# The first sweep of a gated cross-attention block: a listed prologue, a subtraction on GpSimd and a later making of media tiles

## The chip, the cores and the metric

The kernel runs on one core of one Trainium2 chip. The metric is device time in microseconds (us) of one execution, the median of several runs. In what follows PE is TensorE (the matrix engine), DVE is VectorE, ACT is ScalarE, POOL is GpSimd, and SP is the engine that issues most DMAs.

## What is computed

The reference puts four residual blocks behind one another on x of 4 x 1024 x 1024. Only the first matters here, with the layer norm ahead of it:

```python
xb = x.reshape(E, M, K // BLK, BLK)                  # BLK = 128
amax = jnp.max(jnp.abs(xb), axis=-1, keepdims=True)
safe = jnp.maximum(amax, ACT_EPS)
q = (xb * (FP8_MAX / safe)).astype(jnp.float8_e4m3fn)
xq = (q.astype(jnp.float32) * (safe / FP8_MAX)).reshape(E, M, K)
# wq: the same for the media, with one amax for each block of 128 x 128
return jnp.einsum('emk,enk->emn', xq, wq)
...
x = x + jnp.tanh(g_xattn[0]) * _L0_xattn_ref(_layernorm(x, axis=-1), ctx_2048)
```

Both operands of a product of 1024 x 1024 x 1024 (one for each of four batches) are rounded to an 8-bit float and scaled back. Then come a ternary linear layer with an 8-bit activation, whose scale is a maximum over all of x, an attention on the same media, and a layer of eight experts.

## The kernel before, in words

The first sweep (lines 165 to 664) does the first block. It has 32 row tiles of 128 rows of x (class `Rows`, x0 to x31) and 32 media tiles of 128 rows of media, turned (class `Media`, m0 to m31). Eight of each belong to a batch: a row tile of batch b needs all eight media tiles of b, since they hold the output's columns, 128 each.

A **media tile** goes through these steps. `range` is a DVE maximum of each block (L259) and a PE transposition of it (L264). `largest` is a small DVE maximum and a small tensor_scalar (L270, L272) and a PE matmul that spreads the result (L274). `scales` is three or four small DVE instructions (L279 to L285) and one on POOL (L287). Then the tile's sizes: `magnitude` is one ACT instruction (L291), `scale` is eight scaled copies and one Abs on ACT (L221, L230), for tiles that are `scaled`. `round` (function `add`) rounds to the 8-bit float by adding a number of the right size and subtracting it again: k16 by L203 in eight parts or by L197 in one, the sum y by L208 in eight parts (which scales too) or by L199 in one, and last the subtraction, q = y - k16, by L213. `store` writes q, scaled back, into the operand wq: some of the eight blocks by ACT (L237), the rest by DVE (L241). `load` fetches a tile through SP.

A **row tile** has `sum` (ACT, L320), `mean` (DVE, L324), `square` (ACT, L329), `variance` and `range` (DVE L335 and L342, POOL L133 and L347), `scales` (DVE L354, POOL L356 to L358), `scale` (ACT L225 and L230), `round` as above (L197, L199, L213), `restore` (ACT L237 into hd), `transpose` (PE L375), `take` (ACT L381) and `product` in two halves of 512 columns (PE L388, eight matmuls each, which the profile shows as two records each). Then `residual` (DVE L397, which stores x1 and needs the tanh of a gate from `constants`), `spread` (ACT L407), `factor` (DVE L417, POOL L133) and, in every second tile of the first three batches, `extreme` (DVE L426); the other tiles of those come back later (`late_extreme`).

The order on PE, DVE, ACT and POOL is the order in which the program calls these functions: the sweep stands under a manual schedule, and each engine takes its instructions in that order. A prologue (lines 589 to 653) makes up media tiles 0 to 7 in pairs, row tile 0 up to the first half of its product, row tile 1 up to its rounding, and begins row tiles 2 and 3. Then `step(t)` (L517) runs for t = 0 to 31: it does the product of row t, restores row t+1, scales and rounds row t+2, and does the first sums of rows t+3 and t+4. In the first 24 steps it makes up media tile t+8: range and largest one step earlier, scales and round in step t, store in step t+1. PE's `transpose` of the block maxima and its matmul of the largest stand between and behind the halves of the product, so PE waits there for DVE. After step 3 `clear` (L487) fills two buffers by POOL memsets (L490, L495) and writes them out.

Of the first eight media tiles the even ones are scaled; every rounding's subtraction is on DVE; a store of them leaves one of eight blocks to DVE, of the later ones four.

Of the kernel before, what the change touches and what calls it, by code (L numbers as in the profile page):

```python
# [53 lines left out]
def flamingo_kernel(  # L54
# [110 lines left out]
    with ExitStack() as s1:  # L165
# [18 lines left out]
        class Fp8:  # L184


            def tiny(self, name):
                return small.tile(
                    [P, NB], F32, tag=f"{name}{self.name[0]}", name=f"{name}_{self.name}"
                )  # L190

            def add(self, sizes, src, up=None):

                name = self.name
                k16 = w1.tile([P, D], BF16, tag="k16", name=f"k16_{name}", bufs=1)
                if up is None:
                    nc.vector.tensor_scalar(k16, sizes, FP8_LIFT, FP8_FLOOR, ALU.mult, ALU.max)  # L197
                    y = src
                    nc.vector.tensor_tensor(y, src, k16, ALU.add)  # L199
# [12 lines left out]
                self.q = w1.tile([P, D], BF16, tag=f"q{name[0]}", name=f"q8_{name}")  # L212
                nc.vector.tensor_tensor(self.q, y, k16, ALU.subtract)  # L213

            def spread_out(self, src, scale, bias=None):

                name = self.name
                self.y = w1.tile([P, D], F32, tag=f"y{name[0]}", name=f"y8_{name}", bufs=1 + (name[0] == "w"))
# [26 lines left out]
        class Media(Fp8):  # L245


            def __init__(self, t):
                self.t, self.name = t, f"w{t}"

                self.scaled = t < TPB and t % 2 == 0

            def load(self):
                self.c = w1.tile([P, D], F32, tag="c", name=f"c_{self.t}", bufs=4)
# [47 lines left out]
            def store(self):  # L302
                b, hf, j = self.t // TPB, self.t % TPB // NH, self.t % NH
                if (b, hf) not in wqs:
                    wqs[b, hf] = wqp.tile([P, NB, HALF], F32, tag="wq", name=f"wq_{b}_{hf}")
                self.dequantize(wqs[b, hf][:, :, cols(j)], 4 if b else 1)

        class Rows(Fp8):


            def __init__(self, t):
                self.t, self.name = t, f"x{t}"

            def load(self):
                self.x = w1.tile([P, D], F32, tag="x", name=f"x_{self.t}", bufs=6)
# [67 lines left out]
            def product(self, hf):  # L383
# [3 lines left out]
                for k in range(NB):  # L387
# [2 lines left out]
                        start=(k == 0), stop=(k == NB - 1),  # L390
                    )

            def residual(self):
                t = self.t
                self.x1 = w1.tile([P, D], F32, tag="x1", name=f"x1s_{t}")
                tot = small.tile([P, 1], F32, tag="totr", name=f"tot_r{t}")
                nc.vector.scalar_tensor_tensor(  # L397
                    self.x1, self.pm, tg_x0, self.x, ALU.mult, ALU.add, accum_out=tot
                )
                nc.sync.dma_start(x1_dram[t], self.x1)  # L400
                self.mean1 = mean_all[:, t : t + 1]
                nc.vector.tensor_scalar(self.mean1, tot, 1.0 / D, None, ALU.mult)
# [57 lines left out]
        def ternary_scale():  # L460
            tot = small.tile([P, 1], F32, tag="wtot", name="wtot", bufs=1)
            nc.vector.tensor_reduce(tot, part, AX.X, ALU.add)

            spread = w1.tile([P, P], F32, tag="k16", name="wtot_rows", bufs=1)
# [45 lines left out]
        def constants():  # L510
# [3 lines left out]
            nc.scalar.activation(tg, gates, AF.Tanh)  # L514
            nc.scalar.activation(gamma_2, gamma_sb, AF.Square)

        def step(t):  # L517

            near, new, ahead, far, past, old = (at(rows, t + i) for i in (1, 2, 3, 4, -1, -2))
            mp, m, mr, mn = (at(media_t, t + TPB + i) for i in (-1, 0, 1, 3))
# [5 lines left out]
            if t:  # L528
                rows[t].product(0)
            if near:  # L530
                near.restore()
            if mp and t:
                mp.store()
            if ahead:
                ahead.square()
            if past:
                past.residual()
            if mr:
                mr.range()
# [5 lines left out]
            if m:  # L545
                m.scales()
                m.round()
            if old:
                old.factor()
                if old not in waiting:  # L550
                    old.extreme()
# [6 lines left out]
            if mr:  # L558
                mr.largest()
            if past:  # L560
                past.spread()
            if mr:
                mr.magnitude()
            if far:
                far.sum()
            if at(rows, t + 5):
                rows[t + 5].load()
            if mn:
                mn.load()
# [14 lines left out]
            if 5 <= last:  # L584
                for j in range(3 * (last - 5), min(3 * (last - 4), NB)):
                    ternary_block(j)

        with tc.manual_schedule(engines=ORDERED):
# [4 lines left out]
            for r in rows[1:5]:  # L593
                r.load()
            media_t[0].range()
            rows[0].sum()
            rows[0].mean()
            rows[0].square()
            media_t[1].range()
            for m in media_t[0:2]:  # L600
                m.largest()
                m.scales()
            media_t[1].magnitude()
            media_t[0].scale()
            rows[0].variance()
            rows[0].range()
            for i in range(TPB // 2):
                m, n = media_t[2 * i : 2 * i + 2]
                nexts = media_t[2 * i + 2 : min(2 * i + 4, TPB + 1)]
                n.round()  # L610
                if i == 0:
                    rows[0].scales()
                    rows[0].scale()
                elif i == 1:
                    rows[1].sum()
                elif i == 2:
                    rows[1].scales()
                    rows[1].scale()
                else:
                    rows[2].sum()  # L620
                n.store()
                nexts[-1].magnitude()
                for j in nexts:
                    j.range()
                if i in (1, 3):
                    rows[(i + 1) // 2].mean()
                    rows[(i + 1) // 2].square()
                m.round()
                m.store()
                for j in range(2 * i + 4, min(2 * i + 6, TPB + 3)):  # L630
                    media_t[j].load()
                for j in nexts:
                    j.largest()
                if i < 3:
                    for j in nexts:
                        j.scales()
                    nexts[0].scale()
                if i == 0:
                    rows[0].round()
                    rows[0].restore()  # L640
                    rows[0].transpose()
                    rows[0].take()
                elif i == 1:
                    rows[1].variance()
                    rows[1].range()
                    rows[0].product(0)
                elif i == 2:
                    rows[1].round()
                else:
                    rows[2].variance()  # L650
                    rows[2].range()
                    rows[3].sum()
            constants()
            for t in range(NT):
                step(t)
                if t == 3:
                    clear()
# [968 lines left out]
```

## Time and profile before

| | us |
|---|---|
| median of 3 runs | 2051.18 (2050.14 to 2052.25) |
| the profiled execution | 2066.43 |
| its span | 2064.7 |
| PE busy in the span | 1953.8 |
| DVE busy | 1682.4 |
| ACT busy | 1429.4 |
| POOL busy | 600.5 |
| matmuls of the first product (L388), first to last start | 41.8 to 551.8 |

The busy time of an engine is a sum over the whole span; the first sweep is its first quarter. In the lists of single instructions a line gives the start, the duration, engine, line, operation, output and inputs, shape and number; several alike instructions are merged into one line. In the chain of waits a line gives start, length and what the time was spent on. A program's times in the profile come from one execution, which here took longer than the median of the runs.

### The profile page before, as it was taken

Reading aid. Unit: us, or ns where it says so; the run is one execution under the profiler, and the core shown is the slowest. Engines: PE = TensorE matmul, PEld = TensorE weight load, DVE = VectorE, ACT = ScalarE, POOL = GpSimd, SP = SyncE. Lnnn points to the kernel's source line nnn. Section 1 sums busy time; section 2 is a strip of 40 time slices with the busy share of each in tenths; the row PEclk is TensorE's granted clock in tenths of the full one; section 3 lists DMA queues with packets and bytes.
Section 4 is the critical chain, followed back from the end, with each engine's and each line's share of the span. In section 5 each row is a group of like instructions: output and inputs, shape, how many; then the busy total and the mean of one; then the engine's idle time right before and its main releaser. Section 6 shows DMA issues by size and latency. Waiting matters only on the chain.

```text
span 2064.7 us, 24994 instructions
## 1 busy us (share of the span) xinstructions
PE 1953.8 (95%) x7200; PEld 1042.9 (51%) x7200; DVE 1682.4 (81%) x3527; ACT 1429.4 (69%) x2378; POOL 600.5 (29%) x926
## 2 busy tenths in 40 slices
PE   3599999999889999999999999999999999999998
PEld 1244444444334444444444444444444457777766
DVE  8999999988778989898989898989898856555545
ACT  7988988888467776767676777767676645555544
POOL 2234333333100111111212121212121236556664
PEclk9799999999999999999999999999999999999999
DMA  4242332352286767677676767676767865746884
GB/s 173 69 150 98 112 103 92 113 202 102 100 211 159 181 182 182 180 181 187 177 191 174 194 172 194 170 192 172 192 172 184 212 177 195 261 173 212 284 293 162
DMA packets 124751, 357.77 MB, mean 173 GB/s; under 512 B 30583, under 2 KB 38775, under 8 KB 124614
## 3 DMA queue, kind: packets, MB, share of 16 engines
q1 hardware_dynamic: 95094, 271.78, 47.8%
q0 software_dynamic: 29520, 84.39, 12.1%
q8 instruction: 58, 0.95, 0.2%
q14 instruction: 79, 0.65, 0.1%
HBM read 164.08 MB, written 75.61 MB: 116 GB/s over the span
## 4 chain that ended last, share of the span: by engine, by line
PE 86%; DVE 5%; issue 4%; ACT 2%; POOL 2%; DMA 1%; SPq 1%; another core or an unknown queue 0%; POOLq 0%; DVEq 0%; ACTq 0%
PE av L912 21%; PE sc L832 21%; PE mm L388 20%; PE dn L1364 5%; PE f L793 5%; PE up L1374 4%; PE pr L970 3%; PE pt_hmT L960 1%; PE ptx L375 1%; PE pt_hg_acc L1335 1%; PE pt_hg_pt L1335 1%; PE ptq L785 1%; DVE nmax L837 1%; ACT e L841 1%; DVE rmax_w L259 0%
## 5 line engine op out<-in xcount | busy, mean ns | idle before, releaser
L832 PE MATMUL sc<-kv,q 128*128 128x512 f32 x1024 | 488.0, 599 | 4.1 <-ACT q L820 2.4
L912 PE MATMUL av<-eT_x,vT 128*128 128x512 f32 x1008 | 477.3, 596 | 7.7 <-issue 7.5
L388 PE MATMUL mm<-wq,hT 128*128 128x512 f32 x1024 | 454.7, 598 | 0.0
L841 ACT ACTIVATE e<-sc,nmax 128x1024 f32<-128x1024 f32 x256 | 285.3, 1114 | 243.5 <-DVE nmax L837 240.4
L837 DVE TENSOR_REDUCE nmax<-sc 128x1 f32<-128x1024 f32 x256 | 311.9, 1218 | 74.5 <-PE sc L832 74.2
L847 ACT ACTIVATE e<-e,rden 128x1024 f32<-128x1024 f32 x256 | 294.1, 1149 | 58.9 <-DVE rden L844 52.7
L860 DVE STREAM_TRANSPOSE sq<-e 128x1024 f32<-128x1024 f32 x252 | 310.8, 1234 | 0.1
L912 PEld LDWEIGHTS av<-eT_x,vT 128*128 128x128 f32 x1008 | 189.3, 190 | 237.6 <-issue 236.5
L388 PEld LDWEIGHTS mm<-wq,hT 128*128 128x128 f32 x1024 | 191.6, 192 | 220.9 <-issue 217.2
L832 PEld LDWEIGHTS sc<-kv,q 128*128 128x128 f32 x1024 | 185.6, 191 | 182.8 <-issue 169.9
L1364 PEld LDWEIGHTS dn<-hgT,arena_w 128*128 128x128 f32 x1216 | 148.6, 194 | 50.4 <-issue 32.6
L1364 PE MATMUL dn<-hgT,arena_w 128*128 128x128 f32 x1216 | 151.7, 278 | 12.9 <-ACT hgT L1339 10.0
L133 POOL TENSOR_TENSOR rstd_c<-ve_c,neg_half 128x1 f32<-128x1 f32 x31 | 17.7, 570 | 497.4 <-DVE nrm L977 440.8
L1374 PE MATMUL up<-arena_w,ygT 128*128 128x512 f32 x304 | 143.8, 596 | 0.0
L793 PE MATMUL f<-wb_sb 128*128 128x512 bf16 x496 | 117.2, 379 | 2.6 <-DVE y L801 1.4
L1369 ACT COPY ygT<-dn 128x128 f32<-128x128 f32 x76 | 20.3, 267 | 130.0 <-PE dn L1364 97.0
L225 ACT ACTIVATE y_x<-x,off_x,up_x 128x128 f32<-128x128 f32 x256 | 101.5, 479 | 11.5 <-POOL off_x L357 11.5
L237 ACT ACTIVATE hd<-q_x,down_x 128x128 f32<-128x128 bf16 x256 | 78.1, 388 | 21.6 <-DVE q_x L213 21.4
L793 PEld LDWEIGHTS <-wb_sb 128*128 128x128 bf16 x496 | 48.5, 98 | 81.6 <-issue 36.1
L1052 POOL DMA_INDIRECT lists<-token,slot x64 | 66.7, 1042 | 67.3 <-DVE slot L1045 56.8
L133 POOL TENSOR_TENSOR a_all<-va,neg_half 128x1 f32<-128x1 f32 x32 | 36.2, 1131 | 153.1 <-DVE va L417 95.0
L133 POOL TENSOR_TENSOR y<-ve_d,neg_half 128x1 f32<-128x1 f32 x32 | 18.4, 574 | 206.9 <-issue 157.1
(291 smaller groups left out, 2995.5 us busy)
## 6 DMA issues: line engine op xcount, KB each, us to landing
eT_x<-sq SPq DMA_DIRECT2D x1008, 128.0 KB
x<-y SPq DMA_DIRECT2D x32, 514.0 KB
c<-in_ctx_t_dram SPq DMA_DIRECT2D x32, 512.0 KB
x<-in_x_dram SPq DMA_DIRECT2D x32, 512.0 KB
x<-x1s SPq DMA_DIRECT2D x32, 512.0 KB
y<-x SPq DMA_DIRECT2D x32, 512.0 KB
kv<-in_ctx_dram SPq DMA_DIRECT2D x32, 512.0 KB
vT<-in_ctx_t_dram SPq DMA_DIRECT2D x32, 512.0 KB
```

Source lines behind the costliest of these rows:

```text
L225: nc.scalar.activation(self.y[:, cols(k)], src[:, cols(k)], AF.Identity, bias=bias[:, k : k + 1], scale=scale[:, k : k + 1],)
L237: nc.scalar.activation(dst[:, k, :], self.q[:, cols(k)], AF.Copy, scale=down)
L388: nc.tensor.matmul(self.pm[:, hf * HALF : (hf + 1) * HALF], self.hT[:, k, :], wq[:, k, :], start=(k == 0), stop=(k == NB - 1),)
L793: nc.tensor.matmul(po, self.qT[:, k, :], w0T[:, k, cols], start=(k == 0), stop=(k == NB - 1),)
L832: nc.tensor.matmul(sc[:, halves(nh)], qs[t][:, mb * P : (mb + 1) * P], kv[:, halves(nh)], start=True, stop=True,)
L837: nc.vector.tensor_reduce(nmax, sc, AX.X, ALU.max, negate=True)
L841: nc.scalar.activation(self.e, sc, AF.Exp, bias=nmax, accum_out=self.den)
L847: nc.scalar.activation(self.e, self.e, AF.Copy, scale=self.rden)
L860: nc.vector.transpose(sq[:, :, :, j, :], self.e.rearrange("p (k q a) -> p q k a", k=NB, q=4))
L912: nc.tensor.matmul(out_ap, vTs[t][:, k, :], weights, start=(k == 0), stop=(k == NB - 1))
L1364: nc.tensor.matmul(po, self.wa[:, k, :], self.hT[:, k, :], start=(k == 0), stop=(k == NB - 1),)
L1374: nc.tensor.matmul(po[:, halves(hf)], self.yT, self.wb[:, halves(hf)], start=True, stop=True)
```

## The change

There are five parts.

1. The subtraction of a rounding is given to POOL for all row tiles and for media tiles 0 to 7 (`light`). To go with it, k16 has three buffers in place of one and the small tiles four in place of three.
2. Only media tiles 0 and 4 are scaled, and a store of media tiles 0 to 7 leaves two of eight blocks to DVE.
3. A new function `piece(j)` multiplies a row tile with a single media tile. Row tiles 0 and 1 are done by pieces within the prologue, and `step` begins with t = 2. Rows 2 and 3 are rounded in the prologue too.
4. The prologue is a list of 97 items of a fixed order, in which "size" is `scale` or `magnitude` by the tile's kind, a row's "square" has `mean` ahead of it, "range" has `variance`, "scale" has `scales`, and "transpose" has `take` behind it. A media tile's "round" is followed by the load of the tile four further on. Six row tiles are loaded at the start in place of five.
5. Media tiles 8 to 15 are made up in steps 2 to 7: one in steps 2, 3, 5 and 7, two in steps 4 and 6. From step 8 on it is as before.

A row's y lies in an unused part of wb_sb in place of a buffer of its own.

```diff
             def add(self, sizes, src, up=None):
-                k16 = w1.tile([P, D], BF16, tag="k16", name=f"k16_{name}", bufs=1)
+                k16 = w1.tile([P, D], BF16, tag="k16", name=f"k16_{name}", bufs=3)
...
                 self.q = w1.tile([P, D], BF16, tag=f"q{name[0]}", name=f"q8_{name}")
-                nc.vector.tensor_tensor(self.q, y, k16, ALU.subtract)
+                engine = nc.gpsimd if self.light else nc.vector
+                engine.tensor_tensor(self.q, y, k16, ALU.subtract)
...
-                self.scaled = t < TPB and t % 2 == 0
+                self.light = t < TPB
+                self.scaled = t in (0, 4)
...
-                self.dequantize(wqs[b, hf][:, :, cols(j)], 4 if b else 1)
+                self.dequantize(wqs[b, hf][:, :, cols(j)], 4 if b else 2)
...
+            def piece(self, j):
+                if j == 0:
+                    self.pm = ps_m.tile([P, D], F32, tag="mm", name=f"mm_{self.t}")
+                wq = wqs[self.t // TPB, j // NH]
+                for k in range(NB):
+                    nc.tensor.matmul(
+                        self.pm[:, cols(j)], self.hT[:, k, :], wq[:, k, cols(j % NH)],
+                        start=(k == 0), stop=(k == NB - 1),
+                    )
...
+        FIRST = 2
+        media_of = {2: [8], 3: [9], 4: [10, 11], 5: [12], 6: [13, 14], 7: [15]}
+        media_of.update({t: [t + TPB] for t in range(TPB, NT - TPB)})
...
+        PROLOGUE = """
+            m0.range x0.sum m0.largest x0.square m0.scales m1.size m1.range x0.range m0.size x1.sum
+            m1.largest m2.range m1.scales m3.range x3.sum m2.largest x1.square x2.sum x0.scale
+            m0.round m2.scales x1.range m1.round m0.store x2.square m2.size m3.size x0.round
+            m3.largest m4.range m1.store m3.scales m4.largest x0.restore x1.scale x2.range m2.round
+            x0.transpose x3.square m3.round m4.scales p0.0 m5.range m2.store x1.round p0.1 m6.range
+            m4.size x3.range m5.size m5.largest p0.2 x1.restore m3.store x1.transpose p0.3 x2.scale
+            m4.round m6.size m5.scales m6.largest m5.round p1.0 m7.range m4.store m6.scales p1.1
+            m7.largest m7.size p1.2 p1.3 m5.store x2.round p1.4 x3.scale m7.scales p0.4 m6.round
+            m7.round m6.store x4.sum x3.round p1.5 m7.store x4.square p0.5 p1.6 p0.6 x2.restore p1.7
+            p0.7 x5.sum m8.size x2.transpose x4.range m8.range m8.largest
+        """.split()
...
+            for item in PROLOGUE:
+                prepare(item)
             constants()
-            for t in range(NT):
+            rows[0].residual()
+            rows[0].spread()
+            rows[6].load()
+            for t in range(FIRST, NT):
                 step(t)
```

More of the change, by code (lines that the diff above doesn't have):

```diff
@@ L187, in tiny @@
             def tiny(self, name):
-                return small.tile(
-                    [P, NB], F32, tag=f"{name}{self.name[0]}", name=f"{name}_{self.name}"
+                return w1.tile(
+                    [P, NB], F32, tag=f"{name}{self.name[0]}", name=f"{name}_{self.name}", bufs=4
                 )
@@ L212, in add @@
                 self.q = w1.tile([P, D], BF16, tag=f"q{name[0]}", name=f"q8_{name}")
-                nc.vector.tensor_tensor(self.q, y, k16, ALU.subtract)
+                engine = nc.gpsimd if self.light else nc.vector
+                engine.tensor_tensor(self.q, y, k16, ALU.subtract)
             def spread_out(self, src, scale, bias=None):
                 name = self.name
-                self.y = w1.tile([P, D], F32, tag=f"y{name[0]}", name=f"y8_{name}", bufs=1 + (name[0] == "w"))
+                if name[0] == "w":
+                    self.y = w1.tile([P, D], F32, tag="yw", name=f"y8_{name}")
+                else:
+                    self.y = wb_sb[:, 3, :]
                 for k in range(NB):
@@ L305, in store @@
                     wqs[b, hf] = wqp.tile([P, NB, HALF], F32, tag="wq", name=f"wq_{b}_{hf}")
-                self.dequantize(wqs[b, hf][:, :, cols(j)], 4 if b else 1)
+                self.dequantize(wqs[b, hf][:, :, cols(j)], 4 if b else 2)
         class Rows(Fp8):
             def __init__(self, t):
-                self.t, self.name = t, f"x{t}"
+                self.t, self.name, self.light = t, f"x{t}", True
             def load(self):
@@ L462, in ternary_scale @@
             nc.vector.tensor_reduce(tot, part, AX.X, ALU.add)
-            spread = w1.tile([P, P], F32, tag="k16", name="wtot_rows", bufs=1)
+            spread = w1.tile([P, P], F32, tag="k16", name="wtot_rows", bufs=3)
             nc.vector.tensor_scalar(spread, ident, 0.0, tot, ALU.mult, ALU.add)
@@ L515, in constants @@
             nc.scalar.activation(gamma_2, gamma_sb, AF.Square)
+        FIRST = 2
+        media_of = {2: [8], 3: [9], 4: [10, 11], 5: [12], 6: [13, 14], 7: [15]}
+        media_of.update({t: [t + TPB] for t in range(TPB, NT - TPB)})
+        assert sum(media_of.values(), []) == list(range(TPB, NT))
         def step(t):
             near, new, ahead, far, past, old = (at(rows, t + i) for i in (1, 2, 3, 4, -1, -2))
-            mp, m, mr, mn = (at(media_t, t + TPB + i) for i in (-1, 0, 1, 3))
+            mp, ms, mr = ([media_t[i] for i in media_of.get(t + k, [])] for k in (-1, 0, 1))
             last = t - (NT - TPB)
@@ L527, in step @@
                 new.scales()
-            if t:
-                rows[t].product(0)
+            rows[t].product(0)
             if near:
                 near.restore()
-            if mp and t:
-                mp.store()
+            for m in mp:
+                m.store()
             if ahead:
                 ahead.square()
[L536 to L539, printed above, removed]
+            past.residual()
+            for m in mr:
+                m.range()
             if new:
@@ L544, in step @@
                 near.take()
-            if m:
+            for m in ms:
                 m.scales()
+            for m in ms:
                 m.round()
[L548 to L551, printed above, removed]
+            old.factor()
+            if old not in waiting:
+                old.extreme()
             if ahead:
@@ L557, in step @@
             rows[t].product(1)
[L558 to L563, printed above, removed]
+            for m in mr:
+                m.largest()
+            past.spread()
+            for m in mr:
+                m.magnitude()
             if far:
@@ L567, in step @@
                 rows[t + 5].load()
-            if mn:
-                mn.load()
+            for m in ms:
+                if at(media_t, m.t + 4):
+                    media_t[m.t + 4].load()
             if last >= 0:
@@ L586, in step, with prepare @@
                     ternary_block(j)
+        PROLOGUE = """
[10 more added lines that the diff above has]
+        """.split()
+        def prepare(item):
+            what, part = item.split(".")
+            kind, i = what[0], int(what[1:])
+            if kind == "p":
+                rows[i].piece(int(part))
+            elif kind == "m":
+                m = media_t[i]
+                if part == "size":
+                    m.scale() if m.scaled else m.magnitude()
+                else:
+                    getattr(m, part)()
+                if part == "round":
+                    media_t[i + 4].load()
+            else:
+                r = rows[i]
+                for name in {
+                    "square": ("mean", "square"), "range": ("variance", "range"),
+                    "scale": ("scales", "scale"), "transpose": ("transpose", "take"),
+                }.get(part, (part,)):
+                    getattr(r, name)()
         with tc.manual_schedule(engines=ORDERED):
@@ L592, in flamingo_kernel @@
                 media_t[i].load()
-            for r in rows[1:5]:
+            for r in rows[1:6]:
                 r.load()
[L595 to L652, printed above, removed]
```

## The prediction

> **What bounds the kernel now.** I read the windows of 20 us of the first sweep first, to see which engine is full where.
>
> ```profile
> 40.00:60.00 20.00, 11.05 (x26) 5.35 (x26) 18.91 (x56) 16.67 (x47) 5.72 (x10) 0.89 0.16 52
> 60.00:80.00 20.00, 6.76 (x18) 4.05 (x19) 17.51 (x52) 18.70 (x47) 3.77 (x8) 0.51 0.21 59
> 80.00:100.00 20.00, 20.00 (x55) 9.04 (x53) 18.11 (x50) 19.43 (x46) 9.14 (x13) 1.00 0.30 101
> ```
>
> Columns are the stretch, its length, then busy time of PE, PE's weight loads, DVE, ACT and POOL, and PE's granted clock. Until about 74 us PE is mostly idle and DVE and ACT are nearly full. From 80 us on PE is full, and DVE has only 1 to 2 us in 20 to spare.
>
> Then the chain of waits, for the moment at which PE takes over and for a later mark.
>
> ```profile
> 72.50 0.34 POOL amax_x L347
> ...
> 74.20 0.37 PE rmaxT L264
> 74.58 1.71 PE ptx L375 x8
> 76.28 8.57 PE mm L388 x16
> ...
> 100.39 7.06 PE mm L388 x16
> ...
> 176.54 7.06 PE mm L388 x16
> ```
>
> From 74.20 us the chain is PE alone. Row tile 2 starts its product at 100.39 us and row tile 7 at 176.54, 15.23 us a step, without a stall. So the change has 26.2 us of PE time (74.2 to 100.4) to win, and whatever makes PE wait after that to lose. My mark is the start of row tile 7's product: by then media tile 15 is made up in both kernels but for its last step.
>
> Last the timeline of DVE and of POOL at 111 to 130 us, for what the two engines do to each other. DVE:
>
> ```profile
> 111.72 1.23 DVE L199 TENSOR_TENSOR y_x<-y_x,k_x 128x1024 f32<-128x1024 f32 x1
> 112.98 1.22 DVE L213 TENSOR_TENSOR q_x<-y_x,k_x 128x1024 bf16<-128x1024 f32 x1
> ...
> 114.43 0.22 DVE L272 TENSOR_SCALAR spot_w<-ident,top_w 8x8 f32<-8x8 f32 x1
> ...
> 127.94 0.99 DVE L272 TENSOR_SCALAR spot_w<-ident,top_w 8x8 f32<-8x8 f32 x1
> ...
> 128.25 1.86 DVE L241 TENSOR_SCALAR wq<-q_w,down_w 128x128 f32<-128x128 bf16 x4
> ```
>
> POOL:
>
> ```profile
> 111.44 1.76 POOL L133 TENSOR_TENSOR amax_x<-sqmax_x,halves_c 128x8 f32<-128x8 f32 x1 [0.57 <-DVE sqmax_x L342]
> 113.30 1.10 POOL L347 TENSOR_SCALAR amax_x<-amax_x,rstd_a 128x8 f32<-128x8 f32 x1
> ...
> 127.96 0.95 POOL L490 MEMSET wb_sb<- 128x1024 int32 x1
> 128.85 1.11 POOL L495 MEMSET wb_sb<- 128x1028 f32 x1
> ```
>
> When POOL runs two full-width memsets, an 8x8 DVE instruction takes 0.99 us in place of 0.22 and ends with the memset, and the four L241 take 1.86 in place of 0.85. The other way round, POOL's small L347 (0.33 us at 72.50, DVE idle) takes 1.10 when DVE's two-input L213 runs, and ends 0.2 us after it. But DVE's L199 keeps its 1.23 us beside POOL's small power. So a wide POOL instruction stops DVE's tensor_scalar, and a wide DVE one stops POOL.
>
> **The moved subtraction.** It leaves DVE for row tiles and for media tiles 0 to 7: 12 times in the prologue, once a step afterwards. DVE saves 1.24 us each. The trace has no wide two-input POOL instruction. Its nearest row is the 0.95 us memset, which reads nothing; that is the lower end. The Trainium skill, "GPSIMD Engine Reference" (section 3.1), gives an add of 2048 elements 4497 ns on GpSimd and 2293 on DVE, 1.96 times; on the 1.22 us of L213 that is an estimate of 2.4 us. I take 2.3, since the memset doesn't carry the two reads. And its "SBUF — State Buffer" (Who interferes with whom) says the port pair that both engines share is locked for a whole instruction, against DVE's tensor_scalar in its two-port modes and against any DVE instruction with two SBUF inputs. The trace shows the first by the 0.99 us row; for two-input DVE work the small power at 111.44 speaks against a lock of the whole instruction, but it reads only 8 elements. This rule speaks against the change, and I follow it.
>
> **Prologue, DVE's own work** through the storing of media tile 7 (spacing of the rows in the chain). A media tile: range 1.13, largest 0.43, scales 0.81 (0.61 where scaled), round without subtraction 3.52 (13.74 to 17.26) or 1.63 where scaled, two L241 0.5. Tiles 0 and 4 are scaled, six are not: 9.0 + 3.4 + 6.1 + 24.4 + 4.0 = 46.9. Four row tiles: 0.1 + 1.26 + 0.11 + 1.63 = 3.1 each, 12.4. Together 59.3. The first data is there at 4.44, and the first largest, mean and scales leave 1.1 of gaps: 64.8 us without further waits.
>
> **ACT's own work** to the same point: four row scalings 4 x 4.25, two restorations 2 x 2.43, two takings 2 x 1.25, four squares 4 x 1.34, five sums 5 x 1.25, sizes 2 x 3.5 + 6 x 1.04, eight stores of six 8 x 1.83: 63.9. It starts at 5.70; with 3 us of waits for late inputs ACT stores tile 7 at 72.6. Without any lock ACT bounds the prologue, not DVE.
>
> **DVE's waits under the lock**: 12 subtractions of 2.3 are 27.6 us, less the DVE work directly behind each round that needs no shared port. By the list that is 0.6 (media 0), 0.3 (row 0), 0.4 (media 3 and 4), 1.24 (row 1 and media 5, before a range), 0.6 (row 2), and nothing for the other five, where a store, a mean or the next round comes at once: 4.8. So 22.8 us of waits stand against 12 x 1.24 = 14.9 saved. Tile 7 is stored at 64.8 + 22.8 = 87.6. Behind it on ACT stand mean and square of row 4 (1.44), the restoring of row 2 (2.43), a sum (1.25), a size (1.04), the taking of row 2 (1.25) and the gates' tanh (0.2), which row 0's residual waits for: 95.2.
>
> **The pieces.** Sixteen of 8 matmuls each with 128 columns; L1364's 16 records of that shape come in 1.78 us, so 28.5 us for all, in PE time that was idle. Only the last two (3.6, or 7.1 at the clock of 0.51 of 60:80) lie behind tile 7's store; transposition of row 2 comes behind them at 91 to 96, beside the 7.6 of ACT above. I cost them at nothing; uncovered they are 1 to 2 us.
>
> **Steps 2 to 6.** DVE's step with an extreme takes 15.40 (100.12 to 115.52), without 13.52 (85.01 to 98.53). Of it 7.84 is one media tile (range 1.12, scales 0.84, round 4.67, largest 0.44, four L241 0.77) and 1.15 the row's subtraction, so 6.41 and 4.53 remain. Steps 2, 4, 6 and 3, 5: 28.3. They round seven tiles (8 to 14, 38.6), range seven (10.9) and store five (3.9): 53.4. With residual 0 (1.4): 83.1 us of DVE in five steps that give PE 76.1. Two tiles in steps 4 and 6 make DVE the bound. PE waits for the largest in step 6. The row's subtraction holds up the L241 of steps 3 to 6: four waits of 0.5 + 2.3 - 0.6, about 2: 8 us. So row 7 starts at 95.3 + 83.1 + 8 + 0.3 = 186.7 against 176.5: **10.2 us later**.
>
> **Steps 7 to 31.** In a pair of steps DVE now has 28.9 us of PE's 30.46. After it: 28.9 - 2.3 + 2 x 2 = 30.6, at the edge; the largest comes right behind the sum and ahead of the blocked L241, so I take 0. Half a microsecond more a wait would cost 1 us a pair, 8 us to step 23. The row's q reaches ACT 1.7 us later; ACT waits 1.6 us for q and 1.9 for PE in such a step already (114.30, 108.04).
>
> **At nothing**: more buffers for k16 and the small tiles (they let GpSimd lag), the row's y in wb_sb (free until the last steps), a sixth row loaded early (512 KB at some 400 GB/s, 1.3 us on SP's queue, ahead of media loads that wait for a round anyway), the L241 more for each first tile (in the sums). If a media load were late, it would cost about that 1.3.
>
> **Sum.** The profiled execution is 2066.43 us, its span 2064.7; with 10.2 it would be 2076.6. The median of the runs is 15.2 below the profiled one; I carry the difference over: 2051.2 + 10.2 = 2061.4, say 2061.
>
> **Rivals.**
> - *The subtraction is free* (DVE isn't held up by it, as L199 beside the power). Then ACT sets the prologue: 72.6 + 7.6 = 80.2, and row 7 starts at 80.2 + 83.1 + 0.3 = 163.6, 12.9 earlier: 2038. This is the other side; the price of one blocked subtraction decides. At the memset's 0.95 the waits are 7.2, tile 7 is stored at 72.1, under ACT's bound, and the four later waits are 0.85 each: 80.2 + 83.4 + 3.4 = 167.0, so 2042. At 1.6 the waits are 14.4 in the prologue and about 5 later: 64.8 + 14.4 + 7.6 + 83.4 + 5 = 175.2, row 7's old time, so the sign turns near 1.6 us.
> - *In between*: GpSimd and DVE take turns, or DVE slips ahead. Waits of about 12 and 4: within a few us of no change, 2051.
> - *Longer than 2.4* (f32 with bf16 costs more): at 3.3 the prologue loses 12 more, and every later pair of steps 2: some 2085.
>
> **How the numbers follow.** Forecast 0.5 (2056 to 2070), free 0.22, between 0.18, longer 0.1. The range 2039 to 2071 leaves out the last and the far end of the second. A difference under 0.2% (4.1 us) can't be told from none; the cases give faster 0.27, same 0.15, slower 0.58.
>
> **What would show it.** POOL's q rows near 2.3 us; L241, L203 and L197 long behind them; row 2's product near 95, row 7's near 187; PE waiting for the largest (L274) in steps 4 and 6. If q takes 1 us, or L203 stays at 1.39 beside it, I am wrong and the kernel is faster.

## The result, and the profile after

The changed kernel took 2058.78 us (median of 6 runs, 2056.45 to 2060.05) beside 2051.37 for the kernel before (6 runs): ratio 1.003, 95% interval 1.002 to 1.004, or 7.4 us slower. Its profiled execution took 2058.75 us, its span 2057.0.

| start, us | before | forecast | after |
|---|---|---|---|
| product of row 2 | 100.39 | 95.2 | 88.14 |
| product of row 7 | 176.54 | 186.7 | 179.03 |
| transposition of row 8 | 183.6 | | 186.1 |
| last residual of the sweep | 552.40 | 562.6 | 556.74 |

(The forecast's last value is 552.40 + 10.2.) So the listed prologue wins 12.3 us, the next five steps take 14.7 us more than the 76.15 of before, and the rest of the sweep loses another 1.8: 4.3 at its end. All later marks up to 1720 us stand 3.9 to 4.3 us later than before. The other 3 us of the medians have no place in the first sweep, and I come back to them at the end of the experiments.

The windows of after, for the same kind of stretches as before (columns as there: stretch, length, busy time of PE, its weight loads, DVE, ACT, POOL, then PE's granted clock, DMA share and GB/s):

```profile
40.00:60.00 20.00, 12.58 (x86) 11.65 (x86) 19.69 (x50) 15.82 (x41) 11.29 (x12) 0.91 0.18 55
60.00:80.00 20.00, 17.03 (x145) 16.44 (x146) 19.69 (x56) 13.49 (x37) 9.24 (x10) 1.00 0.24 78
...
120.00:140.00 20.00, 18.22 (x43) 8.43 (x43) 19.13 (x62) 12.80 (x30) 6.36 (x10) 0.83 0.59 211
```

DVE has under 1.2 us in 20 to spare from 40 to 180 us, but for the handover to PE at 80 to 100, where it is busy for 15.47 (an instruction that is held up counts as busy). Before, it shared the prologue with ACT and gave way to PE at 80 us. Now ACT has 4 to 8 us in 20 to spare from 40 us on (again but for the handover), and PE's clock, which was 1.00 from 80 us on, falls to 0.83.

The chain of waits, around the handover to PE:

```profile
79.66 0.39 DVE wq L246 x2
...
81.39 2.34 ACT hd L242 x8
...
86.66 0.12 ACT tg L532
86.80 1.30 DVE x1s L415 x2
```

Media tile 7 is stored at 80.0 (forecast 87.6), then come row 2's restoring and the tanh on ACT, and row 0's residual, which releases row 2's product. That is the tail the forecast named, 8.1 us long (forecast 7.6). Where the chain of before was PE alone from 74 us on, this one runs through DVE, POOL and ACT until 425 us, in step 23, and only then is PE.

DVE's timeline, five instructions that wait inside their own duration:

```profile
23.96 3.03 DVE L199 TENSOR_TENSOR wb_sb<-wb_sb,k_x 128x1024 f32<-128x1024 f32 x1
...
36.63 3.33 DVE L203 TENSOR_SCALAR k_w<-size_w,lift_w 128x128 bf16<-128x128 bf16 x8
...
101.98 2.73 DVE L246 TENSOR_SCALAR wq<-q_w,down_w 128x128 f32<-128x128 bf16 x4
...
117.47 3.91 DVE L279 TENSOR_SCALAR spot_w<-ident,top_w 8x8 f32<-8x8 f32 x1
...
157.15 2.13 DVE L279 TENSOR_SCALAR spot_w<-ident,top_w 8x8 f32<-8x8 f32 x1
```

and POOL's beside the first and the last two:

```profile
23.65 2.26 POOL L214 TENSOR_TENSOR q_w<-y_w,k_w 128x1024 bf16<-128x1024 f32 x1
...
117.46 2.12 POOL L214 TENSOR_TENSOR q_x<-wb_sb,k_x 128x1024 bf16<-128x1024 f32 x1
119.52 0.95 POOL L508 MEMSET wb_sb<- 128x1024 int32 x1
120.41 0.96 POOL L513 MEMSET wb_sb<- 128x1028 f32 x1
...
157.14 2.12 POOL L214 TENSOR_TENSOR q_x<-wb_sb,k_x 128x1024 bf16<-128x1024 f32 x1
```

The same instructions take 1.23, 1.39, 0.85, 0.22 and 0.22 when POOL is quiet. The instruction at 23.96 ends 1.1 us after POOL's subtraction (26.99 and 25.91), which is about its own time. An 8x8 product that starts 0.01 us after POOL's subtraction ends with it: 157.14 + 2.12 = 159.26, 157.15 + 2.13 = 159.28. At 117.47 it sits through the subtraction and both memsets of the clearing.

What PE makes of these two, in its timeline:

```profile
88.14 7.13 PE L395 MATMUL mm<-wq,hT 128*128 128x512 f32 x16 [2.19 <-DVE x1s L415]
...
121.44 0.59 PE L281 MATMUL bmax<-spot_w,ones 8*128 8x8 f32 x2 [2.66 <-DVE inv_x L361]
121.96 9.85 PE L395 MATMUL mm<-wq,hT 128*128 128x512 f32 x16
...
159.34 0.59 PE L281 MATMUL bmax<-spot_w,ones 8*128 8x8 f32 x2 [1.97 <-DVE mu_a L331]
159.85 9.68 PE L395 MATMUL mm<-wq,hT 128*128 128x512 f32 x16
...
179.03 7.13 PE L395 MATMUL mm<-wq,hT 128*128 128x512 f32 x16
```

PE waits for the second `largest` of a pair (the profile names another DVE instruction beside the signal; the timeline shows that L279 is what ends then), and the half product behind it takes 9.7 to 9.9 us in place of 7.13. Counted from row t's transposition to row t+1's, step 4 thus takes 21.2 us and step 6 21.3, steps 3, 5 and 7 take 15.3, 16.4 and 16.6. Step 8 takes 15.41, step 9 16.19, and from step 10 to 22 they alternate between 15.23 and 15.50, where all of these were 15.23 before.

### The profile page after: what moved, and what is told of

Same layout as the page of the kernel before. It is cut to its first block, busy times and chain, and to the rows that moved or that the text cites. A ratio compares the mean times of both kernels' runs of the same rounds, so it can differ in the third digit from the quotient of the medians.

```text
span 2057.0 us, 25321 instructions
## 1 busy us (share of the span) xinstructions
PE 1952.1 (95%) x7360; PEld 1059.0 (51%) x7392; DVE 1692.6 (82%) x3525; ACT 1418.9 (69%) x2354; POOL 670.3 (33%) x966
## 4 chain that ended last, share of the span: by engine, by line
PE 68%; DVE 14%; ACT 7%; POOL 5%; issue 5%; DMA 1%; POOLq 0%; DVEq 0%; ACTq 0%
PE av L919 21%; PE sc L839 21%; PE mm L395 6%; PE f L800 5%; PE dn L1371 4%; PE up L1381 4%; PE pr L977 3%; DVE y_w L208 2%; DVE k_w L203 2%; PE pt_hmT L967 1%; DVE wq L246 1%; DVE rmax_w L266 1%; ACT wb_sb L230 1%; ACT hd L242 1%; DVE sqmax_x L349 1%
## 5 line engine op out<-in xcount | busy, mean ns | idle before, releaser
L395 PE MATMUL mm<-wq,hT 128*128 128x512 f32 x960 | 428.1, 601 | 2.2 <-DVE x1s L415 2.2
L395 PEld LDWEIGHTS mm<-wq,hT 128*128 128x128 f32 x960 | 180.2, 192 | 210.8 <-issue 201.1
L230 ACT ACTIVATE wb_sb<-x,off_x,up_x 128x128 f32<-128x128 f32 x256 | 101.6, 479 | 6.6 <-POOL off_x L364 6.6
```

The costliest lines, as they stand in the source:

```text
L230: nc.scalar.activation(self.y[:, cols(k)], src[:, cols(k)], AF.Identity, bias=bias[:, k : k + 1], scale=scale[:, k : k + 1],)
L395: nc.tensor.matmul(self.pm[:, hf * HALF : (hf + 1) * HALF], self.hT[:, k, :], wq[:, k, :], start=(k == 0), stop=(k == NB - 1),)
```

## The experiments

The expectations call their theories A and B anew for each run. The two that I began with: the loss is POOL's hold on DVE (A); or the loss is the new order, above all the steps with two media tiles, and the hold only moves it about (B). "Last residual" is the start of the sweep's last one in the profile (552.4 before, 556.7 after), the sharpest mark of the sweep's length. A mark comes from one execution, and PE's clock moves it: "rows from 4 back" has the prologue of after, but its last pieces ran at a clock of 0.78 (80 to 85 us) where after had 1.00, and row 2's product came 1.0 us later. So a difference of 1 us between two marks says little. The ratio is to runs of the kernel before on the same chip, whose medians were 2051 to 2061 us.

| run | row 2's product | row 7's product | row 8's transposition | last residual | ratio to before |
|---|---|---|---|---|---|
| after | 88.14 | 179.03 | 186.1 | 556.7 | 1.003 [1.002, 1.004] |
| order alone | 85.62 | 176.64 | 186.0 | 554.8 | 1.0026 [1.0017, 1.0035] |
| move alone | | | 193.4 | 563.1 | 1.0061 [1.0048, 1.0074] |
| rows from 4 back on DVE | 89.11 | 179.52 | 189.1 | 558.0 | 1.0047 [1.0034, 1.006] |
| before, again | | | 183.6 | 552.4 | 1.0 [0.9991, 1.0009] |
| store behind | 87.87 | 178.94 | 187.7 | 555.3 | 1.0016 [1.0006, 1.0027] |
| two unrounded | 88.14 | 170.84 | 177.9 | 548.4 | 0.9986 [0.9969, 1.0003] |
| ranges behind | 86.29 | 176.31 | 186.1 | 553.7 | 1.0001 [0.9989, 1.0014] |
| gates early | 89.29 | 180.63 | 190.2 | 558.1 | 1.0034 [1.0022, 1.0046] |
| two scaled on ACT | 88.25 | 177.29 | 184.4 | 554.7 | 1.0017 [1.0008, 1.0025] |
| both | 91.10 | 180.53 | 189.3 | 558.2 | 1.003 [1.0018, 1.0042] |
| both, on ranges behind | 85.51 | 172.68 | 181.5 | 549.1 | 0.9994 [0.9985, 1.0002] |
| largest early | 92.01 | 181.18 | 189.9 | 557.6 | 1.0022 [1.0008, 1.0037] |

**Order alone.** The changed kernel with every subtraction on DVE.

```diff
-                engine = nc.gpsimd if self.light else nc.vector
+                engine = nc.vector
```

> The changed kernel with every rounding's last subtraction on DVE again, all else kept. Theory A (a POOL subtraction of 2.1 us holds DVE's next shared-port instruction up for nearly all of its length): in the prologue DVE gets 12 x 1.22 = 14.6 us of work back and loses the 17.8 us of waits that the changed kernel's trace shows, so row tile 2's product starts near 85 us (88.1 in the changed kernel); steps 2 to 6 get 5 x 1.15 of work and lose 4 waits of 1.9, so row 7 starts near 174 (179.0); later steps go back to 15.23 us. The sweep's last residual starts near 550 (556.7), and the time is near 2050 to 2052, 7 us under the changed kernel. Theory B (the subtraction is a real relief of DVE and the two-tile steps alone cost the time): DVE has 20 us more to do before row 7, so the sweep ends 10 us or more later than in the changed kernel and the time is near 2070.

Measured: the last residual 1.9 us earlier than after, and the time some 5 us above before (ratio 1.0026). Neither theory had this: A had the last residual at 550, B at 567 or later. Row 2's product comes 2.5 us earlier, and the steps from 8 on take 15.23 again. But from row 2's product to row 7's it is 91.0 us, against 90.9 in the changed kernel: there the move of the subtraction gains as much as it costs. PE's timeline:

```profile
117.55 0.68 PE L281 MATMUL bmax<-spot_w,ones 8*128 8x8 f32 x4
...
138.11 0.59 PE L281 MATMUL bmax<-spot_w,ones 8*128 8x8 f32 x2 [4.96 <-DVE mu_a L331]
138.64 9.60 PE L395 MATMUL mm<-wq,hT 128*128 128x512 f32 x16
```

Without POOL's hold the pair's second `largest` is no longer late (x4, no wait). A step later PE waits 4.96 us, because DVE has rounded two media tiles and a row by itself (from 112 to 139 us it waited for only 0.5 us in all). The order alone, without a single subtraction on POOL, is slower than before.

**Move alone.** The kernel before, with the subtractions on POOL and the buffers that go with it.

```diff
...
-                nc.vector.tensor_tensor(self.q, y, k16, ALU.subtract)
+                engine = nc.gpsimd if self.light else nc.vector
+                engine.tensor_tensor(self.q, y, k16, ALU.subtract)
...
```

> The kernel before with nothing changed but the subtraction on POOL for all row tiles and media tiles 0 to 7, with the buffers that go with it. Theory A: ten subtractions in the prologue, and behind nine of them DVE's next instructions are a store that needs the result or a next round, so each costs 2.1 us of wait for 1.22 saved: the prologue ends 6 to 9 us later, and each later step costs 0.1 us or so: the time is near 2060. Theory B: DVE is relieved by 12 us in the prologue, so that row 1 starts earlier, and nothing changes after: the time is 2040 to 2046.

Measured: row 1's transposition 9.6 us later than in before, row 8's 9.8, the last residual 10.7. Theory A is right in kind and too low (6 to 9 us). In the old order a store comes straight behind the round, so DVE isn't only held up by POOL at work, it stands still for POOL's result:

```profile
72.94 0.28 DVE L245 TENSOR_SCALAR wq<-q_w,down_w 128x128 f32<-128x128 bf16 x1 [2.30 <-POOL q_w L214]
```

By the last residual the move costs 10.7 us in the old order and 1.9 in the listed one; the order (with all else that the change brings) costs 2.4 with the subtraction on DVE and wins 6.3 with it on POOL. The two parts of the change don't add up.

**Rows from 4 on back on DVE.**

```diff
-                self.t, self.name, self.light = t, f"x{t}", True
+                self.t, self.name, self.light = t, f"x{t}", t < 4
```

> The changed kernel with the subtraction back on DVE for row tiles 4 to 31 only, so that the prologue is untouched. Theory A: row 2 starts at 88.1 as in the changed kernel, row 7 about 2 us earlier (177), and the steps from 8 on take 15.23 us in place of 15.37, another 1.8 us by step 23: the last residual starts near 553, some 4 us before the changed kernel's, and the time is near 2055. Theory B (the subtraction relieves DVE in the steps): steps 2 to 6 get 5.8 us longer, and the time is near 2064.

Measured: the steps from 8 on take 15.23. That alone shows little, for row 8 comes 3 us later than in after, and a late row gives DVE time: gates early (below), with its subtractions on POOL and row 8 at 190.2, has 15.23 from step 8 to 22 too. But order alone, with the subtraction on DVE, and ranges behind (below), with the store moved away from it, have 15.23 with row 8 within 0.2 us of after's. So what after loses there, 3.0 us in steps 8 to 23, is the row's subtraction with L246 behind it, as at 101.98. Ahead of rows 5 and 7 PE waits for 4.96 and 4.48 us; nothing is won in sum (from row 2's product to the last residual 468.8 us, 468.6 in after).

**Before, again.**

> The kernel before, unchanged, for a second profile. In the two profiles the sweep's end and all marks to 1720 us lie 3.9 to 4.3 us apart, but the medians 7.4; the profiled execution of before was 15 us over its median. Theory A (the experts' units at the end take a length that varies from execution to execution): the last residual starts at 552.4 again, and the stretch from 1720 us to the end is some 10 us shorter than the first profile's. Theory B (the profile lengthens this kernel throughout): all marks shift in proportion.

Measured: the last residual at 552.4 as in the first profile, the stretch from the last marks of the third block to the end 348.1 us, against 360.0 in the first profile of this same kernel and 348.4 in the changed kernel's. The 12 us by which the first profiled execution was long lie there, and have nothing to do with the change.

**Store behind.** DVE's four blocks of a media tile's store put behind the residual and the ranges, so that the subtraction of the row meets work that it didn't hold up in after's trace: a range took 1.21 us beside a subtraction at 47.60, as without one.

```diff
...
-                m.store()
+                m.store("act")
...
                 m.range()
+            for m in mp:
+                m.store("dve")
```

> The changed kernel with one thing moved: in every step DVE's part of a media tile's store (the four L241, now L249) comes behind the row's residual and the next media tile's range, which need no port that POOL uses, in place of ahead of them. All subtractions stay where they are. Theory A (what the moved subtraction costs in the steps is that a store stands right behind it): the store no longer waits, so DVE gets 1.6 us back in each of steps 3 to 6, where DVE is the bound, and the steps from 8 on go back from 15.36 to 15.23 us. Row 8's transposition starts near 180 (186.1 in the changed kernel), the last residual near 547 (556.7), and the time is 2048 to 2051. Theory B (POOL's subtraction delays the row's q for ACT, and that delay sets the later steps): the steps from 8 on stay at 15.36 and the last residual is within 2 us of 556.7, or 4 us earlier by steps 3 to 6 alone.

Measured on a chip where before took 2061 us: all steps from 8 on at 15.23, as expected, but the last residual only 1.4 us earlier. In step 2 the half clock came:

```profile
87.87 10.02 PE L397 MATMUL mm<-wq,hT 128*128 128x512 f32 x16 [2.19 <-DVE x1s L417]
```

The wait is the 2.19 us that the changed kernel has at 88.14, where the product took 7.13 at a clock of 1.00; here the clock was 0.50 from 88 to 92 us. DVE then waited 2.8 us for this product, and a wait of 4.95 came ahead of row 7's product. So this run doesn't measure what the moved store alone is worth in steps 2 to 7.

**Two unrounded.** Media 11 and 14 are only copied to bf16: their rounding is left out.

```diff
-                if self.scaled:
+                if self.t in (11, 14):
+                    self.q = w1.tile([P, D], BF16, tag="qw", name=f"q8_{self.name}")
+                    nc.vector.tensor_copy(self.q, self.c)
+                elif self.scaled:
```

> The changed kernel, in which media tiles 11 and 14, the second ones of steps 4 and 6, are only copied to bf16 and not rounded to the 8-bit float: this leaves out 4.67 us of DVE in each of these two steps, puts some 0.65 us in its place, and leaves all else. Theory A (in steps 4 and 6 DVE is the bound because of the second tile, and that eats what the prologue wins): row 8's transposition starts 8 us or more earlier, at 175 to 178, steps 4 and 6 take some 17 us in place of 21.2, and the last residual starts at 546 to 549. Theory B (the time goes in waits for POOL or for ACT, not for DVE's own work): less than 3 us.

Measured: row 8's transposition 8.2 us earlier, last residual 8.4; the copies took 0.68 us each for a rounding of 4.67, so 8.0 us of DVE work were left out. The wait of 2.65 behind the clearing is still there, the later ones are gone:

```profile
155.07 0.61 PE L281 MATMUL bmax<-spot_w,ones 8*128 8x8 f32 x4
155.61 7.13 PE L398 MATMUL mm<-wq,hT 128*128 128x512 f32 x16
```

though POOL held the second `largest` up in this step too:

```profile
152.99 2.13 DVE L279 TENSOR_SCALAR spot_w<-ident,top_w 8x8 f32<-8x8 f32 x1
```

With DVE ahead by one rounding the same hold costs PE nothing. This is the run that decides: DVE's work is 8.0 us less and the sweep 8.4 us shorter, so from row 2 to row 7 the bound is DVE's sum of work and holds, and single waits of PE only show where it surfaces.

**Ranges behind.** On the kernel "store behind": five ranges of the prologue's list are put behind roundings whose subtraction would otherwise meet work that it holds up (m4.range behind m1.round, x2.range behind m2.round, m5.range behind m3.round, x3.range behind m4.round, m8.range behind x2.round).

> As the kernel with the stores behind the ranges, and the prologue's list rearranged so that a block maximum (range), which needs no shared port, comes right behind five more of the twelve subtractions: media 4's behind media 1's round, row 2's behind media 2's, media 5's behind media 3's, row 3's behind media 4's, media 8's behind row 2's. Theory A: each hides 1.1 us of DVE's 17.8 us of waits in the prologue, row 2's transposition starts 4 to 5 us earlier than the 83.8 of the changed kernel, unless ACT holds it (its bound is near 77), and the last residual starts near 543; the time is 2044 to 2047. Theory B (ACT or POOL bound the prologue already): no earlier than the kernel with only the stores moved.

Measured: row 2's product at 86.3. DVE was done 4.1 us before it could take row 0's residual, for the tanh of the gates on ACT. Of what the ranges won, 1.9 us were left at row 2's product (against after), and the half clock behind it (8.77 us for 7.13) took 1.6 of these.

**Gates early, two scaled on ACT, both, and both on ranges behind.** Gates early puts two loads and the tanh into the prologue and row 0's residual directly behind its last piece; two scaled makes media 11 and 14 `scaled` tiles.

```diff
-            m4.round ...   x4.sum ...   p0.7 x5.sum
+            m4.round g0.gates ...   x4.sum g0.tanh ...   p0.7 x0.residual x5.sum
...
-                self.scaled = t in (0, 4)
+                self.scaled = t in (0, 4, TPB + 3, TPB + 6)
...
```

> The changed kernel, with the gates loaded and their tanh taken during the prologue (at the fifth row sum) in place of behind it, and row 0's residual put directly behind the last piece of row 0's product, ahead of row 4's range and the ninth tile's range and largest. In the changed kernel the product of row 2 starts at 88.1 us and is released by row 0's residual, which itself waited 1.28 us for the tanh. Theory A (the handover from the prologue waits for this one residual, and the later steps keep their lengths): row 2's product some 4 us earlier (near 84), all later rows as much earlier, last residual near 553 instead of 556.7, total 4 us below the changed kernel (ratio to the kernel before about 1.001). Theory B (what is saved at the handover comes back as a longer wait for a 'largest' of a double step, as it did when the moved subtraction was given back to VectorE in the prologue): row 2's product earlier, but row 8's transposition within 1 us of where it was, total unchanged (ratio 1.003).

> The changed kernel, with the second tile of each pair (media 11 and 14) scaled by ScalarE instead of by VectorE, in steps 4 and 6: VectorE loses 8 block operations of two kinds for single wider ones in each of them (about 2 us), ScalarE gains about 2.5 us. Theory A (the double steps are bound by VectorE's own work, and ScalarE has room for more than that: 12.5 to 15.8 of each 20 us are busy there): steps 4 and 6 shorten by 2 us or a little more each, last residual near 552.5 instead of 556.7, ratio to the kernel before about 1.001. Theory B (VectorE then waits for ScalarE's scaling, because ScalarE has the row's restoring and the store ahead of it): steps 4 and 6 stay within 0.5 us of 21.2 and 21.3, with VectorE's wait for the scaled tile or its sizes in place of its work; ratio 1.003.

> Both edits of this call together on the changed kernel. Theory A (the two losses add up, each being on the chain of VectorE): last residual near 549, ratio to the kernel before about 0.999, the first version below it. Theory B (each gain is taken back by the other's wait): last residual near 555, ratio 1.002 to 1.003.

> Both edits of this call on the kernel with the store's VectorE part put behind residual and range and the prologue's ranges behind the five roundings. That kernel lost 4.1 us to the tanh at row 0's residual, and its steps from 8 on took 15.23 us. Theory A: row 2's product 4 us earlier, steps 4 and 6 2 us shorter each, last residual near 546 (it was 553.7 there), ratio to the kernel before about 0.997: the best of all. Theory B (early time is turned into waits of TensorE of 3 to 5 us, with half clock after them): last residual near 552, ratio 1.000.

Gates early failed, and for a reason that neither theory had:

```profile
88.07 0.27 PE L271 MATMUL rmaxT<-ident,rmax_w 128*8 128x128 f32 x1 [3.07 <-DVE rmax_w L266]
...
89.29 8.83 PE L395 MATMUL mm<-wq,hT 128*128 128x512 f32 x16
```

With the residual ahead of media 8's range on DVE, that range is late, and its transposition and the matmul of its `largest` stand ahead of row 2's product in PE's queue. Two scaled gave 2.0 of the 4 us that were expected: steps 4 and 6 themselves did not get shorter (21.2 and 21.7), the holds at the second `largest` being ahead of them, and steps 5 and 7 gave 0.8 and 1.4. On the changed kernel the two together gave nothing (last residual 558.2); on "ranges behind", where media 8's range comes early, they gave 4.6, so that the sweep ends 3.3 us ahead of before. Its ratio, 0.9994, can't be told from 1. No run was clearly faster than the kernel before.

**Largest early.** On the last one, media 8's `largest` straight behind media 7's rounding, and the clearing's memsets at the start of the sweep.

```diff
-            m7.round m6.store ...   x4.range m8.largest
+            m7.round m8.largest m6.store ...   x4.range
```

> The kernel with store and ranges behind, gates early and media 11 and 14 scaled by ScalarE, with two more edits: the ninth tile's largest directly behind the eighth tile's rounding, so that its small matmul no longer stands between the last pieces and row 2's product, and the two memsets of the clearing (0.95 us each on GpSimd, in step 3, where VectorE's small product for the largest took 3.91 us for 0.22) at the start of the sweep, where GpSimd is idle from 2.7 to 7.8 us. Theory A (TensorE's own queue held row 2's product: 2.40 us for the small matmul, and the half clock after it made the product's first half 8.56 us long in place of 7.1; and the memset's hold on the shared port cost step 3 2 us): row 2's product near 83 instead of 85.5, step 3 back to 15.3, last residual near 545 instead of 549.1, ratio to the kernel before about 0.998. Theory B (time won before a double step comes back as a longer wait there, since VectorE's work of these steps is unchanged): row 8's transposition within 1 us of 181.5, last residual near 549, ratio 0.9994 as before the two edits.

Measured: the memsets' part of the hold is gone (the second `largest` of step 3 takes 2.14 us for 3.91). PE doesn't wait ahead of row 4's product, and step 4 takes 15.45; but step 3 had taken 19.0 in place of 15.3, which gave DVE time, so it isn't shown which of the two took the wait away. The time comes back in step 5, which takes 21.3 in place of 18.1, as theory B has it. And row 2's product comes 6.5 us later:

```profile
76.29 0.59 PE L283 MATMUL bmax<-spot_w,ones 8*128 8x8 f32 x2 [7.66 <-DVE spot_w L281]
76.81 13.66 PE L408 MATMUL mm<-wq,hT 128*128 128x128 f32 x96
```

I had moved the DVE half of `largest` with care and its PE half without. DVE could make this `largest` only behind tile 7's rounding, and POOL's subtraction held it up as well; its small matmul, ahead of the last 12 pieces in PE's queue, held them all up. In "both, on ranges behind" nearly 6 of the 12 are done by 75.9 us. After the wait of 7.66 us the clock was 0.50 from 76 to 80 us besides.

**The forecasts of these runs.** In ten of them theory A named the last residual. It came in once, in two unrounded (548.4 in 546 to 549); the other nine times it came 2 to 13 us later than A had it. What a single edit wins at its own place was lost again, in whole or in part, at a later one.

**The other 3 us.** Over the twelve changed kernels the median moved by 1.2 us less to 3.1 us more than the last residual did (on average 1.2 more). The changed kernel is at the upper end. That part of its 7.4 us I can't locate; it may be no more than the spread. The interval of the ratio, 4 to 8 us, reaches down to about the 4.3 of the sweep, and the spans of the second profile of before and of after, 2052.7 and 2057.0, differ by just these 4.3.

## Why the prediction was right, point by point

The forecast was 2061 (+10.2); the runs gave 2058.8 (+7.4), in the range and with the likeliest sign. The total is better than its parts.

- *The subtraction on POOL*, taken at 2.3: 2.13 (median of 40), 1.74 times DVE's 1.22. The estimate from the factor of 1.96 in the Trainium skill, "GPSIMD Engine Reference" (section 3.1), was 2.4; the measurement decides.
- *The hold lasts for the whole instruction, against tensor_scalar and two-input DVE work alike*: right in the main. L199 with two SBUF inputs took 3.03, 1.80 more than alone, so the row of before that spoke against it, the small power at 111.44, was no guide. But not every tensor_scalar is held up: those of one column (L331, 128x1) took their usual 0.15 us beside a subtraction, ten times in after.
- *Waits in the prologue*, 22.8: mis-sized. Ten of the twelve subtractions held DVE up, by 1.04 to 1.95 us each, 17.8 in sum. The duration took 2 us off; one subtraction (row 3's, at 79.80) began only when tile 7's store was under way and held up nothing of it, another 2; and one (at 47.60) held up nothing, where I had counted about 1.
- *DVE's own work to tile 7's store*, 64.8: 80.0 - 17.8 = 62.2. Small counts were too high: `scales` takes 0.71 (0.81 in the sum), two L246 0.39 (0.5). Together with the waits this is the term of the sum that was mis-sized most: tile 7 came at 80.0, not 87.6, and row 2's product 7.1 us ahead of the forecast.
- *The tail on ACT*, 7.6: 8.1, ended by the tanh as foretold. *The pieces at nothing*: they hid; PE was waiting for row 0's residual again from 85.95.
- *Steps 2 to 6*, 83.1 of DVE and 8 of waits, 91.5 to row 7's product: 90.9. The sum was right (the four holds were 9.3 in sum), and two unrounded shows why a sum over DVE is the right tool here. The places were not all right: I had the holds only at the store's L246, and two of the four, of 3.7 and 1.9 us, were at the second `largest` of a pair, straight ahead of work in PE's queue.
- *Steps 7 to 31 at nothing*: 1.8 us from row 7's product to the last residual. Steps 8 to 23 lose 3.0 by the subtraction ahead of L246 (order alone and ranges behind both bring 15.23 back); from step 24 on 1.2 of it come back. "At the edge" was right, but the cost was 0.19 us a step on average and not 0.
- *The sum*: row 7 came 2.5 us later than before, where I had 10.2. The prologue's cost was overrated by 7.1 us; 1.8 of later steps and the 3 us that no mark shows made the total look closer than it was. The sign and the mechanism, DVE's work and holds in the steps of pairs, were right; that +7.4 is so near to +10.2 is in part luck. Two slips of the working carry no weight: PE was busy for 11.05 of the 20 us from 40 us on, so not mostly idle there, and the sum starts row 2 at 95.3 where the tail gave 95.2.
- *The rivals*: "the subtraction is free" put the prologue's end at 80.2 and the gain at 12.9 us. With no hold at all (order alone, the subtraction on DVE) the sweep was 2.4 us slower than before. That isn't the free POOL subtraction, which no run has: order alone leaves 12 subtractions in the prologue and one a step on DVE. It shows that without any hold, too, the steps with two media tiles take what the prologue wins, as long as DVE does all the work; what a free subtraction would give stays open.

## What to carry to other kernels

An operation that is given to another engine is paid for by what stands directly behind it in the order of the engine it left: list those instructions one by one, and ask of each whether a trace shows it held up beside the other engine. Where one engine is the bound over several steps, sum its work and its holds over all of them; a single wait that is taken away there comes back at the next place, as it did in order alone, store behind and largest early. And an item of a hand-written order puts instructions on several queues at once, so that an earlier place on DVE can be a roadblock on PE.

## What the hardware showed unasked

PE's granted clock falls after short waits. The window of 4 us behind the 2.66 us wait of after (its clock is the third number from the end):

```profile
122.00:126.00 4.00, 4.00 (x6) 1.81 (x6) 3.76 (x14) 4.00 (x12) 0.98 (x4) 0.50 1.01 404
```

The clock is 0.50 here, 0.75 from 126 to 129 and 1.00 again from 129 us; from 111 to 118, ahead of the wait, it was 1.00. Over after and eleven experiments I sorted the half products from 85 to 182 us by the longest wait ahead of them. Of 11 with 0.66 to 1.45 us none was slow (7.11 to 7.13); of 11 with 1.84 to 2.19 seven were (8.77 to 10.15); of 22 with 2.4 to 4.96 all but one (8.56 to 10.15).

Inside or beside most of these waits PE runs a tiny matmul of 0.3 to 0.6 us. Counted from the end of the last matmul of full size, as if PE stood idle in the tiny ones (and without the one case of move alone, which has a transposition in between), the order is cleaner: of 10 up to 2.08 us none was slow, of 17 from 2.16 to 3.31 eleven were, of 16 from 3.48 on all. The Trainium skill, "TensorE: Matmul & The Clock Gate" (Part 1: The HAM clock gate), lets PE fall to half after at least one idle window of some 3.4 us that runs freely. The last group agrees with that; but 2.16 us can't fill such a window and were enough at times, and there the measurement decides. Why the middle is mixed no run here shows.

A slow half product costs 1.4 to 3.0 us beside the wait, where PE sets the pace. Where DVE does, as at 121.96 and 159.85 in after, the chain of waits runs through DVE and not through the slow product.
